# Decoder on one core: the first feed-forward with three batches open, its scratch stores on GpSimd, its norm on ScalarE and half of its rounding on VectorE

## The chip, the cores and the metric

The program is one kernel on one core of a Trainium2 chip. A core has a matrix engine (TensorE; PE in the profile, with its weight loads as PEld), three engines for elementwise work (VectorE = DVE, ScalarE = ACT, GpSimd = POOL), and SyncE (SP), which here only issues transfers. SBUF is the memory on the core that all engines read; PSUM holds eight banks of 128 x 512 fp32 into which TensorE writes; HBM is reached by DMA, which any engine but TensorE and VectorE issues here. Each engine runs its own instructions in one fixed order and waits on semaphores where it needs another's result.

The metric is device time in microseconds (us) of one execution. Each kernel is run several times, and the median counts. Besides, one execution is recorded by the hardware profiler; the views of that record are called the profile or the trace.

## The reference

A decoder of two layers on four batches of 512 tokens of width 512, in fp32. Each layer is attention, cross-attention and a feed-forward, and after each of them `x = layernorm(x + f(x))`. The change lies in the first layer's feed-forward (and in when the weights of the next attention are loaded):

```python
def act_quant(x):                       # per token, 8 bits
    scale = 128 / clip(max(abs(x), axis=-1), 1e-5)
    return clip(round(x * scale), -128, 127) / scale
def weight_quant(w):                    # ternary
    scale = 1 / clip(mean(abs(w)), 1e-5)
    return clip(round(w * scale), -1, 1) / scale
def bitlinear(x, w):   return einsum('bsh,oh->bso', act_quant(x), weight_quant(w))
def h_bitlinear(x, w): return einsum('bsh,oh->bso', act_quant(fwht(x)), weight_quant(w))
gate = bitlinear(x, w_gate)             # 512 -> 2048
up = bitlinear(x, w_up)                 # 512 -> 2048
x = layernorm(x + h_bitlinear(silu(gate) * up, w_down))   # 2048 -> 512
```

`fwht` is a normalised Walsh-Hadamard transform over the 2048 columns. `setup_inputs` makes random activations and weights.

## The kernel before

**Stages and order.** Six phases, A to F, are first attention, first cross-attention, first feed-forward (C, `l0_ffn`, L546), second attention (D), second cross-attention (E) and second feed-forward (F). Each runs on four batches 0 to 3; the result of a phase goes to HBM and the next phase loads it. Each phase of a batch is a generator that issues a few instructions and then yields. `lanes` (L1111) interleaves them: it takes the generators in the order A0 A1 ... F3 (L34), keeps at most two open, and opens the next when the last one opened has said "next" and the same batch has finished the phase before. Beside the named phases, `BESIDE` (L36) runs generators that prepare weights: while C3 and D0 are open, `l1_attn_weights` loads 16 `w1` tiles of the next attention's weights on SP, splits each into a high and a low part (ScalarE L135, VectorE L138) and folds a bias through TensorE (`bo1`).

The program's order of issue is then an input to a scheduler that fixes each engine's order of instructions; semaphores and the turn of the buffers (pools of 69 `o`, 13 `t`, 12 `x` and 4 `w` tiles of 256 KB, eight PSUM banks) are placed by it as well. A `Pipe` inside a generator delays a piece: `later(2, f)` calls `f` two ticks on, a tick being one step of the loop.

**One batch of the first feed-forward.** Names are those of the profile's rows.

1. Load four `x` tiles of 128 tokens; the maxima of each token and its scales go into a small tile `cm` (two buffers). Quantise (`qf` on ScalarE L569, `q` on VectorE), transpose to `qT`, and make `arow`, the row of token scales.
2. The front: 16 steps `o`, each a block of 128 hidden columns. A step has the matmuls of gate `pg` and up `pu` (four each, L624 and L626), then `g = pg * arow` (VectorE L595), silu (ScalarE L596), `g = pu * g` (VectorE L600), the split into `hh` (ScalarE L602) and `hl` (GpSimd L603), the first half of the Hadamard transform, a matrix product over the block's 128 columns with `hh` and then `hl` (L608 and L609, into `ph`), and a copy `hw` on ScalarE (L614). Two ticks later SP stores `hw`, 256 KB, to a scratch area in HBM (L615). There are two scratch areas, for even and odd batches. After step 6 the generator says "next".
3. The reload: after all 16 stores, 16 loads `z` on SP read the scratch with columns in another order (`z` number c takes 8 columns of each of the 16 blocks), so every load needs every store.
4. The back: for each of four token tiles, four groups of four matmuls `had` (the transform's second half, L692), each needing four `z`; the maximum of each group (VectorE L638) and a copy `q2f` (ScalarE L640); the scales, small operations on VectorE and one on GpSimd; rounding on ScalarE (L658), a subtraction and clip on VectorE (L659, `q`); eight transposes into `q2T` (L665), a copy (ScalarE L670), and the down product, 16 matmuls `dn` (L678); then the residual and the statistics of the layernorm on VectorE (L682).
5. `finish` (L180): the inverse root in small operations on VectorE (`ln_rsqrt`), `norm` on VectorE (L186), and the store of `x` on SP (L189). All six phases use it.

In the order that results, the fronts of batches 0 and 1 run, then both reloads, both backs; then the same for batches 2 and 3. The four last `dn` of batch 3 come before the second attention's score matmuls (`ds`, L835), which begin at 816.95 us.

**Lines that the change and the prediction touch.** L526 and L527 round weights (`tw`) on VectorE. Rows of the profile write out<-in: `had<-had,z` (L692) is the second half, `ph<-hh,had` the first.

Of the kernel before, what the change touches and what calls it, by code (L numbers as in the profile page):

```python
# [16 lines left out]
AF = mybir.ActivationFunctionType  # L17
ALU = mybir.AluOpType
# [4 lines left out]
P = 128  # L23
NT = 4
MAGIC = 12582912.0
RSQRT_SEED = float(0x5F3759DF)
O_BUFS, T_BUFS, X_BUFS, W_BUFS = 69, 13, 12, 4


D_NEXT = 7  # L30
B_NEXT = 13
F_LOAD = 5
# [32 lines left out]
class Net:  # L65
# [114 lines left out]
    def finish(self, pipe, ys, ln, phase, b):  # L180

        nc = self.nc
        self.ln_rsqrt(ln)

        def norm(i):
            nc.vector.tensor_scalar(ys[i], ys[i], ln[:, 2 * i : 2 * i + 1], ln[:, 24 + i : 25 + i], ALU.subtract, ALU.mult)  # L186

        def store(i):
            nc.sync.dma_start(self.xd[phase + 1][b, i * P : (i + 1) * P, :], ys[i])  # L189

        for i in range(NT):
            pipe.later(3, norm, i)
            pipe.later(4, store, i)
# [352 lines left out]
    def l0_ffn(self, b):  # L546
        nc = self.nc
        pipe = Pipe()
# [2 lines left out]
        yield  # L551
        yield

        cm = self.s("cm", 40, 2)
        am, a1, sc, cs, f2 = (cm[:, 4 * n : 4 * n + 4] for n in range(5))
        for i in range(NT):
            nc.vector.tensor_reduce(am[:, i : i + 1], x[i], AX.X, ALU.max, apply_absolute_value=True)
# [9 lines left out]
        for i in range(NT):  # L567
            f = self.t("qf")
# [22 lines left out]
        scratch = self.had_scratch[b % 2]  # L591
# [20 lines left out]
        def keep(o, ph):  # L612
            w = self.t("hw")
            nc.scalar.copy(w, ph)  # L614
            pipe.later(2, lambda: nc.sync.dma_start(scratch[o * P : (o + 1) * P, :], w))  # L615

        tern = self.tern
        for o in range(16):
            pipe.tick()
            c, m = o // 4, slice((o % 4) * P, (o % 4) * P + P)  # L620
            self.need("C", lambda: (3, c) in tern["wu_t"])
            pg, pu = self.pa("pg"), self.pa("pu")
            for k in range(NT):
                nc.tensor.matmul(pg, tern["wg_t"][k, c][:, m], qT[k], start=k == 0, stop=k == NT - 1)  # L624
            for k in range(NT):
                nc.tensor.matmul(pu, tern["wu_t"][k, c][:, m], qT[k], start=k == 0, stop=k == NT - 1)  # L626
            pipe.later(1, gate, o, pg, pu)
            yield "next" if o == 6 else None
        yield from pipe.drain()

        z = [self.load(self.o("z"), scratch.rearrange("(i c b) t -> c i b t", i=16, c=16)[c]) for c in range(16)]
        ln = self.ln_tile()
        yield
        yield
# [19 lines left out]
        def quant(i, half, fs, s2):  # L654
            q = self.t("q2", BF16, 1024)
            for g in range(2):
                f = fs[half * 2 + g]
                nc.scalar.activation(f, f, AF.Copy, bias=MAGIC, scale=s2)  # L658
                nc.vector.tensor_scalar(q[:, g * 512 : g * 512 + 512], f, MAGIC, 127.0, ALU.subtract, ALU.min)  # L659
            pipe.later(2, turn, i, half, q)  # L660

# [40 lines left out]
    def l1_attn_weights(self):  # L702
        nc, a = self.nc, self.a
# [13 lines left out]
        f = self.w("after")  # L717
# [6 lines left out]
        pipe = Pipe()  # L724
# [5 lines left out]

        for c, k, ap in order:
            pipe.tick()
            pipe.later(1, put, c, k, self.load(self.w("w1"), ap))
            yield
        yield from pipe.drain()

# [15 lines left out]
    def l1_attn(self, b):  # L752
# [75 lines left out]
        def scores(hh):  # L828
            q3, k3 = st.pop((0, hh)), st.pop((1, hh))
            p01, p2, p3 = self.pa("ds"), self.pa("ds"), self.pa("ds")  # L830
            place = ((p01, 0), (p01, 256), (p2, 0), (p3, 0))
            tiles = []
            for i, (ps, o) in enumerate(place):
                w = max(256, P * (i + 1))
                nc.tensor.matmul(ps[:, o : o + w], q3[:, i * P : (i + 1) * P], k3[:, 0:w], start=True, stop=True, skip_group_check=True)  # L835
                tiles.append(ps[:, o : o + P * (i + 1)])
            pipe.later(1, soft, hh, tiles)
# [47 lines left out]
        for hh in range(16):  # L885
# [5 lines left out]
            scores(hh)  # L891
            yield "next" if hh == D_NEXT else None
        yield from pipe.drain()
# [217 lines left out]
def lanes(order, task, step):  # L1111

    todo = [(e.strip("+!"), e[0] == "+", max(1, e.count("!"))) for e in order]
    plain = [name for name, _, _ in todo]
    live, done = {}, set()
    n, said = 0, 9
    while todo or live:
        if todo and len(live) < 2:  # L1120
            name, soon, times = todo[0]
            before = chr(ord(name[0]) - 1) + name[1]
            if (before in done or before not in plain) and (said >= times or not live or soon):
                todo.pop(0)
                live[name] = task(name)
                last = name
                n, said = n + 1, 0
        for name, g in list(live.items()):
            word = next(g, "end")
            if word == "end":  # L1130
                live.pop(name)
                done.add(name)
            elif word == "next" and name == last:
                said += 1
        step(n)
# [91 lines left out]
```

## Time and profile before

| | |
|---|---|
| median of 3 runs | 1662.6 us (1662.27 to 1663.54) |
| profiled execution | 1662.88 us, of it 1660.9 us from the first to the last instruction |
| mean granted TensorE clock | 0.978 of full speed |
| HBM read, written | 112.0 MB, 41.9 MB |

The first feed-forward runs from 479 to 799 us. Busy time of each engine in it and in the first part of the attention that follows, in us (the four stretches between 566 and 759 us that are not in this table are shown in the prediction):

| from-to, us | length | PE | DVE | ACT | POOL | granted clock | GB/s | what runs |
|---|---|---|---|---|---|---|---|---|
| 479-566 | 87 | 84.61 | 59.55 | 68.64 | 41.78 | 1.00 | 172 | fronts of batches 0 and 1 |
| 599-619 | 20 | 20.00 | 18.12 | 16.44 | 0.82 | 1.00 | 17 | backs of batches 0 and 1 |
| 759-799 | 40 | 39.29 | 28.81 | 29.36 | 7.84 | 1.00 | 56 | backs of batches 2 and 3 |
| 799-880 | 81 | 79.45 | 52.86 | 68.66 | 29.44 | 1.00 | 104 | second attention |

How to read it: the busy time of PE is modelled, since matmuls overlap, and an engine counts as busy while an instruction of it is open, so a full PE may still be doing its work at less than its peak. The granted clock is the share of TensorE's full clock that the chip allowed in that stretch. A row such as `pg<-qT,tb 128x512 bf16 x4` is a run of four instructions; the figures before it are its start and duration, and what stands in brackets behind it is the idle time before it and the work that ended that idle time. A DMA issue has two durations: that of the issuing instruction, and the time until the data landed. Over the stage, stores of `hw` have an issue of 0.32 us (median) and land 2.0 us after it; a `z` load lands 6.6 us after its issue (median, the 16 of a batch being queued together).

Mean durations of one instruction over the whole trace, for the operations that the change moves or that stand beside them:

| row | mean, ns | count |
|---|---|---|
| ACT L658 rounding `q2f` | 745 | 64 |
| DVE L659 `q<-q2f` | 419 | 64 |
| POOL L603 `hl` | 1323 | 64 |
| ACT L614 `hw` copy | 590 | 64 |
| DVE L186 `norm`, all phases | 687 | 96 |
| ACT L602 `hh` | 621 | 64 |

### The profile page before, as it was taken

To read this page: it belongs to the slowest core of one execution; us is meant where nothing else is said; L and a number is where in the kernel's file an instruction comes from. 1 tells how busy PE (TensorE), PEld (TensorE's weight loads), DVE (VectorE), ACT (ScalarE), POOL (GpSimd) and SP (SyncE) were. 2 spreads that over 40 slices of the span, in tenths; PEclk is the share of its full clock that TensorE was granted. 3 is DMA by queue.
4 is the path that set the end of the run, shared out by engine and by line. 5 is a ranking of instruction groups with operands and counts; after the bars stand their busy time and mean duration, and the time that the engine had idled before them with its cause. 6 is when DMAs were issued, how large, how long until landed. Compare 5 with 4: busy or idle time off the path is not lost.

```text
span 1660.9 us, 25661 instructions
## 1 busy us (share of the span) xinstructions
PE 1549.7 (93%) x8246; PEld 1110.3 (67%) x8246; DVE 1267.4 (76%) x2796; ACT 1007.5 (61%) x2149; POOL 667.4 (40%) x672
## 2 busy tenths in 40 slices
PE   7999999999999899899999999999988889999995
PEld 5888775444544674466777767777667766786874
DVE  6386688999976678876565675756879999979795
ACT  5333326888778867786696865968533445444542
POOL 5663653555535203420435332343323344333332
PEclk9999998999999999999999999999998999999998
DMA  7043343455114634763433323333444532021000
GB/s 243 28 146 121 127 133 118 144 165 184 58 71 146 193 114 138 205 188 98 127 77 77 77 64 109 83 77 77 153 152 123 189 106 63 9 69 47 5 26 25
DMA packets 103237, 180.77 MB, mean 109 GB/s; under 512 B 16560, under 2 KB 18608, under 8 KB 103104
## 3 DMA queue, kind: packets, MB, share of 16 engines
q1 hardware_dynamic: 98976, 170.69, 32.8%
q0 software_dynamic: 4128, 8.46, 2.1%
q8 instruction: 65, 1.06, 0.3%
q14 instruction: 68, 0.56, 0.1%
HBM read 111.98 MB, written 41.94 MB: 93 GB/s over the span
## 4 chain that ended last, share of the span: by engine, by line
PE 54%; DVE 23%; ACT 9%; DMA 7%; issue 4%; POOL 2%; SPq 1%; DVEq 0%; ACTq 0%; POOLq 0%
PE fg L1080 7%; PE facc L1071 6%; DVE bsm L413 3%; PE dT L857 2%; ACT de L847 2%; PE pu L626 2%; PE pg L624 2%; DVE x L186 2%; DMA z<-had_scratch 2%; DVE fg L1044 2%; PE dn L678 2%; PE dq L146 2%; PE dq L147 2%; PE dq L148 2%; PE do L877 2%
## 5 line engine op out<-in xcount | busy, mean ns | idle before, releaser
L1044 DVE SCALAR_TENSOR_TENSOR fg<-fg,gs,fg 128x512 f32<-128x512 f32 x220 | 162.4, 745 | 36.8 <-PE fg L1080 17.5
L1080 PE MATMUL fg<-fxh,gu 128*128 128x512 f32 x352 | 144.2, 410 | 7.5 <-DVE fg L1044 4.6
L847 ACT ACTIVATE de<-de,dm 128x128 f32<-128x128 f32 (+3 forms) x256 | 143.0, 563 | 13.4 <-DVE dm L846 12.4
L846 DVE CUSTOM_DVE_ANT_0 de<-ds,negm,thr 128x128 f32<-128x128 f32 (+3 forms) x256 | 126.5, 546 | 31.0 <-PE ds L835 27.9
L421 POOL TENSOR_SCALAR be<-be,bsm 128x512 f32<-128x512 f32 x128 | 95.7, 760 | 120.5 <-DVE bsm L419 70.4
L1080 PE MATMUL fg<-fxl,gu 128*128 128x512 f32 x352 | 139.2, 395 | 0.0
L603 POOL TENSOR_TENSOR hl<-g,hh 128x512 fp32r<-128x512 f32 x64 | 84.2, 1323 | 114.6 <-ACT hh L602 93.4
L1048 POOL TENSOR_TENSOR fg<-fg,fg 128x512 f32<-128x512 f32 x44 | 61.0, 1387 | 128.4 <-ACT fg L1041 69.5
L415 ACT ACTIVATE be<-bs,bsm 128x512 f32<-128x512 f32 x128 | 87.5, 690 | 39.3 <-DVE bsm L413 32.3
L777 POOL TENSOR_TENSOR dql<-dqf,dqh 128x512 fp32r<-128x512 f32 x32 | 41.4, 1295 | 154.5 <-ACT dqh L776 120.8
L857 PE MATMUL dT<-ident,de 128*128 128x128 f32 x640 | 89.9, 278 | 7.9 <-ACT de L847 5.9
L1080 PEld LDWEIGHTS fg<-fxh,gu 128*128 128x128 f32 x352 | 67.3, 191 | 38.1 <-DVE fg L1044 14.2
L857 PEld LDWEIGHTS dT<-ident,de 128*128 128x128 f32 x640 | 71.7, 141 | 25.6 <-ACT de L847 14.4
L1038 ACT ACTIVATE fg<-fg,gs 128x512 f32<-128x512 f32 x88 | 60.4, 686 | 39.1 <-PE fg L1080 38.6
L413 DVE TENSOR_REDUCE bsm<-bs 128x1 f32<-128x512 f32 x128 | 84.0, 674 | 0.1
L692 PE MATMUL had<-had,z 128*128 128x128 f32 x512 | 75.0, 293 | 9.5 <-DMA z<-had_scratch 9.3
L692 PEld LDWEIGHTS had<-had,z 128*128 128x128 f32 x512 | 68.9, 203 | 17.1 <-issue 6.4
L1071 PE MATMUL facc<-p4h,fhh 128*128 128x512 f32 x176 | 71.7, 409 | 8.9 <-DVE fg L1044 6.2
L437 PE MATMUL bo<-bpT,cT 128*64 128x512 f32 x256 | 75.4, 625 | 3.5 <-ACT bpT L428 1.5
L199 PEld LDWEIGHTS bT<-ident,be 128*128 128x128 f32 x512 | 55.1, 141 | 34.4 <-issue 12.9
L199 PE MATMUL bT<-ident,be 128*128 128x128 f32 x512 | 73.7, 283 | 3.9 <-POOL be L421 1.4
L1041 ACT ACTIVATE fg<-fg,gs 128x512 f32<-128x512 f32 x44 | 30.2, 687 | 75.1 <-PE fg L1080 75.1
(330 smaller groups left out, 4715.8 us busy)
## 6 DMA issues: line engine op xcount, KB each, us to landing
x<-x SPq DMA_DIRECT2D x176, 256.0 KB, 3.1
had_scratch<-hw SPq DMA_DIRECT2D x64, 256.0 KB, 2.0
z<-had_scratch SPq DMA_DIRECT2D x64, 256.0 KB, 6.6
stk<-dqh SPq DMA_DIRECT2D x192, 64.0 KB, 2.1
tw<-in_wg_t SPq DMA_DIRECT2D x32, 256.0 KB, 4.1
tw<-in_wu_t SPq DMA_DIRECT2D x32, 256.0 KB, 3.5
tw<-in_wd_t SPq DMA_DIRECT2D x32, 256.0 KB, 2.7
p<-in_gu_p SPq DMA_DIRECT2D x22, 256.0 KB, 2.7
```

The costliest lines, as they stand in the source:

```text
L199: self.nc.tensor.transpose(pt[:, i * P : (i + 1) * P], srcs[i][:, j * P : (j + 1) * P], self.ident)
L413: nc.vector.tensor_reduce(sm[:, h : h + 1], ps, AX.X, ALU.max, negate=True)
L415: nc.scalar.activation(e, ps, AF.Exp, bias=sm[:, h : h + 1], accum_out=sm[:, 2 + h : 3 + h])
L421: nc.gpsimd.tensor_scalar(es[h][i], es[h][i], sm[:, 4 + h : 5 + h], 1.0, ALU.mult, ALU.mult)
L603: nc.gpsimd.tensor_tensor(lo, g, hi.bitcast(F32), ALU.subtract)
L692: nc.tensor.matmul(ps[:, c * P : (c + 1) * P], z[g * 4 + c][:, i * P : (i + 1) * P], self.had16, start=True, stop=True)
L846: nc.vector.tensor_tensor_reduce(es[i], ps, self.negm[:, 384 - P * i :], -1.0, self.thr[:, i : i + 1], ALU.add, ALU.min, n4[:, i : i + 1])
L847: nc.scalar.activation(es[i], es[i], AF.Exp, bias=n4[:, i : i + 1], scale=-1.0, accum_out=den[:, hh * 4 + i : hh * 4 + i + 1])
L857: nc.tensor.transpose(pt[:, o + (i - j) * P : o + (i - j + 1) * P], es[i][:, j * P : (j + 1) * P], self.ident)
L1044: nc.vector.scalar_tensor_tensor(y[u], ps, s, y[u], ALU.mult, ALU.add)
L1071: nc.tensor.matmul(acc[t], h[l][:, c], self.dn[i][r], start=i == 0 and n == 0, stop=i == 10 and n == 2)
L1080: nc.tensor.matmul(ps, self.gu[i, u][:, g * P : (g + 1) * P], xT[g][n], start=n == 0, stop=n == 1)
```

## The change

In the first feed-forward:

- `lanes` lets three generators be open while the next one to open is a C; otherwise two, as before. The front says "next" after step 9 rather than 6.
- `finish` of this phase computes -mean x rstd for the four tiles in one small VectorE operation and normalises on ScalarE (`x * rstd + (-mean * rstd)`); the store of the result is issued by ScalarE rather than SP.
- The stores of `hw` to the scratch are issued by GpSimd rather than SP, one tick after the copy rather than two.
- Of the two halves of each token tile's rounding, the first runs on VectorE (multiply and add in one instruction) rather than ScalarE.
- `cm` has three buffers rather than two.

And the 16 `w1` loads of the next attention's weights are placed behind the latest `z` load in SP's order.

The changed order has the same instructions otherwise: 64 stores go from SP to GpSimd, 16 from SP to ScalarE, 16 norms from VectorE to ScalarE, 32 roundings from ScalarE to VectorE, and four small VectorE operations are new.

```diff
--- before.py
+++ after.py
@@ -27,6 +27,9 @@
 O_BUFS, T_BUFS, X_BUFS, W_BUFS = 69, 13, 12, 4
 
 
+C_NEXT = 9
+
+NORM_ACT = (2,)
 D_NEXT = 7
 B_NEXT = 13
 F_LOAD = 5
@@ -182,11 +185,19 @@
         nc = self.nc
         self.ln_rsqrt(ln)
 
+        on_act = phase in NORM_ACT
+        if on_act:
+
+            nc.vector.scalar_tensor_tensor(ln[:, 28:32], ln[:, 0:8].rearrange("p (i two) -> p i two", two=2)[:, :, 0], -1.0, ln[:, 24:28], ALU.mult, ALU.mult)
+
         def norm(i):
-            nc.vector.tensor_scalar(ys[i], ys[i], ln[:, 2 * i : 2 * i + 1], ln[:, 24 + i : 25 + i], ALU.subtract, ALU.mult)
+            if on_act:
+                nc.scalar.activation(ys[i], ys[i], AF.Identity, bias=ln[:, 28 + i : 29 + i], scale=ln[:, 24 + i : 25 + i])
+            else:
+                nc.vector.tensor_scalar(ys[i], ys[i], ln[:, 2 * i : 2 * i + 1], ln[:, 24 + i : 25 + i], ALU.subtract, ALU.mult)
 
         def store(i):
-            nc.sync.dma_start(self.xd[phase + 1][b, i * P : (i + 1) * P, :], ys[i])
+            (nc.scalar if on_act else nc.sync).dma_start(self.xd[phase + 1][b, i * P : (i + 1) * P, :], ys[i])
 
         for i in range(NT):
             pipe.later(3, norm, i)
@@ -551,7 +562,7 @@
         yield
         yield
 
-        cm = self.s("cm", 40, 2)
+        cm = self.s("cm", 40, 3)
         am, a1, sc, cs, f2 = (cm[:, 4 * n : 4 * n + 4] for n in range(5))
         for i in range(NT):
             nc.vector.tensor_reduce(am[:, i : i + 1], x[i], AX.X, ALU.max, apply_absolute_value=True)
@@ -612,7 +623,7 @@
         def keep(o, ph):
             w = self.t("hw")
             nc.scalar.copy(w, ph)
-            pipe.later(2, lambda: nc.sync.dma_start(scratch[o * P : (o + 1) * P, :], w))
+            pipe.later(1, lambda: nc.gpsimd.dma_start(scratch[o * P : (o + 1) * P, :], w))
 
         tern = self.tern
         for o in range(16):
@@ -625,10 +636,11 @@
             for k in range(NT):
                 nc.tensor.matmul(pu, tern["wu_t"][k, c][:, m], qT[k], start=k == 0, stop=k == NT - 1)
             pipe.later(1, gate, o, pg, pu)
-            yield "next" if o == 6 else None
+            yield "next" if o == C_NEXT else None
         yield from pipe.drain()
 
         z = [self.load(self.o("z"), scratch.rearrange("(i c b) t -> c i b t", i=16, c=16)[c]) for c in range(16)]
+        self.reload = self.loaded
         ln = self.ln_tile()
         yield
         yield
@@ -655,7 +667,10 @@
             q = self.t("q2", BF16, 1024)
             for g in range(2):
                 f = fs[half * 2 + g]
-                nc.scalar.activation(f, f, AF.Copy, bias=MAGIC, scale=s2)
+                if half:
+                    nc.scalar.activation(f, f, AF.Copy, bias=MAGIC, scale=s2)
+                else:
+                    nc.vector.tensor_scalar(f, f, s2, MAGIC, ALU.mult, ALU.add)
                 nc.vector.tensor_scalar(q[:, g * 512 : g * 512 + 512], f, MAGIC, 127.0, ALU.subtract, ALU.min)
             pipe.later(2, turn, i, half, q)
 
@@ -730,7 +745,8 @@
 
         for c, k, ap in order:
             pipe.tick()
-            pipe.later(1, put, c, k, self.load(self.w("w1"), ap))
+            with self.tc.issue_after(self.reload.ins):
+                pipe.later(1, put, c, k, self.load(self.w("w1"), ap))
             yield
         yield from pipe.drain()
 
@@ -1117,7 +1133,7 @@
     live, done = {}, set()
     n, said = 0, 9
     while todo or live:
-        if todo and len(live) < 2:
+        if todo and len(live) < (3 if todo[0][0][0] == "C" else 2):
             name, soon, times = todo[0]
             before = chr(ord(name[0]) - 1) + name[1]
             if (before in done or before not in plain) and (said >= times or not live or soon):
```

## The prediction

> **What bounds the kernel now.** I read the totals first, then the busy time by stretch of the first feed-forward (the only stage whose instruction order the change moves, apart from its seam with the attention that follows), then TensorE's timeline there, then the chain of waits at the two holes.
>
> ```profile
> PE 1549.7 (93%) x8246; PEld 1110.3 (67%) x8246; DVE 1267.4 (76%) x2796; ACT 1007.5 (61%) x2149; POOL 667.4 (40%) x672
> ```
>
> TensorE is the busiest engine, but its busy time is modelled, so I count its work from rows instead. The stage runs from 479.5 us (first gate matmul) to 798.6 us (last down matmul), 319.1 us.
>
> ```profile
> core 0: us, PE busy (x) PEld busy (x) DVE busy (x) ACT busy (x) POOL busy (x), PEclk, DMA share, GB/s
> 566.00:599.00 33.00, 27.63 (x173) 20.15 (x172) 17.40 (x45) 21.21 (x35) 0.85 (x3) 0.84 0.53 153
> 619.00:705.00 86.00, 77.81 (x383) 39.47 (x382) 75.12 (x148) 65.10 (x113) 33.76 (x26) 0.98 0.57 178
> 705.00:729.00 24.00, 24.00 (x156) 16.53 (x156) 20.31 (x42) 19.46 (x37) 10.80 (x10) 1.00 0.64 204
> 729.00:759.00 30.00, 25.87 (x161) 18.72 (x160) 16.13 (x40) 19.77 (x33) 0.56 (x2) 0.89 0.61 169
> ```
>
> The reader is to see two stretches in which every engine falls back at once, GpSimd to nothing, and the granted clock drops to 0.84 and 0.89. Between them TensorE is full beside DVE at 85%. What a piece of work costs TensorE is the distance from one start to the next where nothing waits:
>
> ```profile
> 497.85 1.04 PE L624 MATMUL pg<-qT,tb 128*128 128x512 bf16 x4
> ...
> 500.04 1.04 PE L624 MATMUL pg<-qT,tb 128*128 128x512 bf16 x4
> ...
> 603.29 3.62 PE L678 MATMUL dn<-tb,q2T 128*128 128x512 bf16 x16
> 606.74 0.61 PE L665 MATMUL q2T<-ident,q 128*128 128x128 bf16 x8
> 607.19 2.90 PE L692 MATMUL had<-had,z 128*128 128x128 f32 x24
> 609.92 3.62 PE L678 MATMUL dn<-tb,q2T 128*128 128x512 bf16 x16
> ```
>
> One front step (gate, up, first Hadamard half) is 2.19 us, a tile of `dn` 3.45, eight transposes 0.45, eight records of `had` 0.91. Four batches: 64 x 2.19 = 140.2, 64 x 0.91 = 58.2, 16 x 3.45 = 55.2, 32 x 0.45 = 14.4; `arow` and `qT` of three batches 5.5, the bias fold `bo` 4.2 (697.50 to 701.73), attention work let in at the end 4.6. Sum 282.3, so about 37 of 319 us are lost. The same count inside the stretches (88 `had`, 48 `dn`, 40 transposes in the first hole, 22.6 us of work in 33) gives 10.4 us lost in the first, 9.4 in the second and 11.9 in 619 to 705.
>
> ```profile
> 572.27 3.42 DMA had_scratch<-hw
> ...
> 578.24 5.39 DMA z<-had_scratch
> ...
> 583.70 7.46 DMA z<-had_scratch
> 591.16 0.14 issue
> ```
>
> The holes are the round trip through scratch: the last store of a batch lands, only then its 16 loads start.
>
> ```profile
> 575.75 11.27 SPq L203 DMA_DIRECT2D z<-had_scratch  x16
> ...
> 579.24 0.77 PE L692 MATMUL had<-had,z 128*128 128x128 f32 x2 [3.92 <-DMA z<-had_scratch]
> ```
>
> First load issued 575.75, first `had` 579.24 (3.5 us), sixteenth load used at 594.75: one load per (594.75 - 579.24) / 15 = 1.03 us. Both batches of a pair have finished their fronts by then, so nothing is left to run.
>
> **The change part by part.** The sum is made against the profiled execution, 1662.9 us (span 1660.9 and 2.0 around it); the median is 1662.6.
>
> *Three batches open, "next" at step 9.* In the changed order on TensorE, `had` of batch 0 stands between steps of batch 1, that of batch 1 between steps of batch 2, that of batch 2 between steps of batch 3. The pair's common hole goes: -10.4 and -9.4. Of the 11.9 us in 619 to 705, 5.5 stand around the bias fold (TensorE waits 2.90 us before 697.50, DVE splitting attention weights) and stay, since the fold still falls into batch 3's front; the other 6.4 are the restart of two fronts on drained engines, which now happens inside another batch's back: -6.4. Together -26.2. The later "next" costs nothing: batch 1's first step stands after batch 0's last Hadamard halves, and at 512 to 517.8 TensorE already waits there for `qT`.
>
> *What it adds there.* Four reloads instead of two pairs. From the last Hadamard matmul to the last of 16 loads: matmul and copy 0.25 + 0.1 + 0.6, store 2.3 with issue, first load 3.5, fifteen more 14.3 to 15.5: 21.4 us taken. Batch 0's reload stands beside five steps of batch 1 (5 x 1.74 = 8.7 us before the first `had`, against 6.8 for the first load), then a group of four loads takes 3.8 to 4.1 us where a step with its `had` group takes 3.1: +2 (0 to 7). Batch 1's has about 13 us of batch 2's steps before its first `had`: 0 (0 to 4). Between batch 2's last half and batch 3's first gate matmul TensorE's order holds 4.5 of `had`, two `dn` (6.9), 40 transposes (2.3), `arow` and `qT` (1.9): 15.6 against 21.4, +6 (0 to 10). After batch 3's last half stand one `dn` (3.45) and `had` of two tiles (7.3) before the attention's first transpose: 10.8 against 21.4 and 2 for the second tile, +12.6 (8 to 17).
>
> *The seam.* Attention's first transpose then comes with about 17 us more of batch 3's back still to do than before. Two of its four `dn` with their transposes (2 x 3.9) stand among the score matmuls of 817 to 880, where TensorE loses 2 to 5 us in each 10; they are hidden there: -7 (0 to -8). If that cover is gone they cost 7.
>
> *GpSimd issues 64 stores.* No 256 KB store from GpSimd is in the trace. Its `had` load of 64 KB took 0.74 us of the engine and landed after 2.29; the 32-partition copies took 0.50. Bounds 0.50 and four times 0.74, 2.95; taken 0.8, by the row with 128 partitions. 51 us go onto an engine that has 95 of 318 busy: hidden, because a store and a split (0.8 + 1.28) stay under a step of 2.19. At 2.95 they don't, and the split `hl` behind a store, which the Hadamard matmul waits for, sets a step of 4.2. SP loses 64 issues of 0.32; loads no longer hold stores back as at 542.29 to 546, where a store waits for landings of loads. That block had no TensorE cost of its own: 0 (0 to -3).
>
> The DMA issue itself comes second. The Trainium skill (DMA: Bandwidth & Descriptors, "Issuing engine by pattern") gives simple stores to Sync, and states about 1 us to the first byte for GpSimd against 0.6. The rows above have 2.29 against 2.0 to landing. By the page's difference the four last stores would cost 4 x 0.4 = 1.6 us, by the rows 4 x 0.3; neither is in the sum.
>
> *Half of the rounding on DVE, norm on ScalarE, its stores too.* 32 roundings leave ScalarE (0.72 each, median of L658, -23.0) and go to DVE at 0.48, the row of `tw` L526, the same multiply and add (+15.4). 16 norms leave DVE (1.92 / 4 = 0.48, -7.7) for ScalarE at 0.72, the rounding's form (+11.5); 16 issues on ScalarE, none in this trace, by SP's rows 0.32 to 0.72, taken 0.34 (+5.4). ScalarE -6.1, DVE +7.7; both have over 75 us spare in the stage, so 0 by themselves. The issues wait for their norm with the next copies queued behind, and for their semaphore's earlier load: bounds 0 and 11.5.
>
> *DVE beside GpSimd.* This speaks against the change. The same four norms:
>
> ```profile
> 616.78 1.92 DVE L186 TENSOR_SCALAR x<-x,ln 128x512 f32<-128x512 f32 x4
> ...
> 647.47 2.86 DVE L186 TENSOR_SCALAR x<-x,ln 128x512 f32<-128x512 f32 x4
> ```
>
> ```profile
> 643.23 3.02 POOL L603 TENSOR_TENSOR hl<-g,hh 128x512 fp32r<-128x512 f32 x2 [2.02 <-ACT hh L602]
> 648.28 1.31 POOL L603 TENSOR_TENSOR hl<-g,hh 128x512 fp32r<-128x512 f32 x1 [2.02 <-ACT hh L602]
> ```
>
> GpSimd is idle beside the first and splits beside the second: 0.24 us more each. Backs so far ran mostly with GpSimd idle; now 64 `q`, 32 roundings and small steps run beside splits: 96 x 0.24 = 23 us of DVE. That is covered by DVE's spare 80 us except in batch 3's stretch, where 12 weight splits share DVE (about 65 us of DVE to 67 of TensorE): +3 (0 to 23).
>
> The Trainium skill (GPSIMD Engine Reference, "Key points") says that GpSimd shares its SBUF interfaces with VectorE, with contention for DVE instructions that use both ports or read two SBUF operands. The rows agree. The page has no price; by it alone every such pair would contend, at the rows' price the 23 us.
>
> *The rest.* Weight loads behind a reload and a third `cm` buffer move no TensorE work: 0 (-2 to +4).
>
> Sum: -26.2 + 2 + 0 + 6 + 12.6 - 7 + 3 = -9.6, **1653 us**.
>
> **Rivals.** (a) *Reload paces TensorE's fixed order in all four batches: slower.* For it: a hole's loads already run at 1.03 us each with no other traffic, and now another batch's stores share the DMA. With a group of loads at 4.8 us, batches 0 to 3 lose 7, 4, 10 and 17: 38 instead of 20.6. 1662.9 - 26.2 + 38 - 7 = 1668. It decides where a group takes over 4.2 us, a step with its share of the back (2.19 + 0.91 + 3.45/4 + 0.22). Against: 705 to 729 moves 204 GB/s with TensorE full. (b) *The hole only moves to batch 3 and DVE binds its stretch: no change.* DVE's contention at 13 instead of 3: 1663. Against: DVE at 85% in 705 to 729 costs nothing. (c) *Reloads hidden better:* batch 2's under batch 1's `dn`, batch 3's at its lower bound, the rest 0: 1662.9 - 26.2 + 8 - 7 = 1638.
>
> **How the numbers follow.** Main case 0.46, with a range of its own of 1645 to 1661; (a) 0.27; (b) 0.13; (c) 0.14. I predict 1653; the range 1636 to 1676 reaches into (c) and past (a) by its last bound. A measurement of this kernel tells 0.2% (3.3 us) from no change. Faster: 0.41 of the main case and (c), with a little of (b): 0.56. Same 0.13. Slower 0.31, from (a) and the edges of (b).
>
> **What would show it.** TensorE without a hole while batches 1 and 2 run their fronts; `had` of batch 2 and of batch 3 waiting on `z`, about 6 and 12 us; GpSimd's stores near 0.8 us; `q` and the roundings 0.2 us longer beside `hl`; attention's first transpose near 770 us and its score matmuls a few us earlier than 817. Wrong would be: `had` waiting on `z` in all four batches, GpSimd setting the step, or score matmuls later than 817 with TensorE stopped behind DVE or ScalarE.

## The result, and the profile after

The changed kernel takes 1712.0 us (median of 4 runs, 1711.7 to 1713.1) beside 1663.1 us for the kernel before; the ratio is 1.0288, with a 95% interval of 1.0269 to 1.0308. It is slower by about 48 us. The prediction was 1653 us with a range up to 1676: wrong in sign and in size. The profiled execution took 1713.1 us, of it 1711.4 us from the first to the last instruction, at a mean granted clock of 0.967 (0.978 before).

The totals of the changed kernel, from the page:

```profile
PE 1579.3 (92%) x8246; PEld 1121.0 (66%) x8246; DVE 1281.3 (75%) x2816; ACT 997.1 (58%) x2133; POOL 707.2 (41%) x736
```

TensorE has the same 8246 matmuls as before and 50.5 us more span (1711.4 - 1660.9). No engine became full: the time went into waits. Four stretches of the changed kernel, between its first gate matmul of the feed-forward (482 us) and the attention's first score matmul (842 us):

```profile
core 0: us, PE busy (x) PEld busy (x) DVE busy (x) ACT busy (x) POOL busy (x), PEclk, DMA share, GB/s
...
600.00:640.00 40.00, 40.00 (x248) 24.38 (x247) 31.58 (x71) 26.53 (x46) 17.20 (x20) 1.00 0.50 156
640.00:680.00 40.00, 28.39 (x176) 19.57 (x174) 25.50 (x64) 23.63 (x41) 9.66 (x13) 0.86 0.71 214
680.00:720.00 40.00, 33.46 (x198) 21.78 (x198) 31.36 (x73) 27.21 (x45) 7.52 (x8) 0.84 0.36 106
...
760.00:800.00 40.00, 30.14 (x150) 19.85 (x147) 18.38 (x46) 16.44 (x28) 8.35 (x12) 0.79 0.63 204
```

The first of the two holes of before is gone, as meant: TensorE is full from 600 to 640, and it was not in 566 to 599 before. But there are two others, longer ones, at 640 to 720 and at 760 to 800, again with a lower granted clock (down to 0.79). What TensorE waited for between 479 and 930 us (in all, times, longest):

```profile
engine line waited for: us in total, times, longest us
PE had L707 <- DMA z<-had_scratch: 16.7, 15, 6.1
PE dn L693 <- ACT q2T L685: 8.8, 1, 8.8
PE bo L761 <- DVE bvp L758: 3.5, 1, 3.5
PE q2T L680 <- DVE q L674: 2.4, 1, 2.4
```

Two stretches show how. The first, after batch 2's last Hadamard half, as the timeline has it (start, duration, engine; in brackets the wait before):

```profile
643.22 0.82 ACTq L200 DMA_DIRECT2D x<-x  x2
...
645.30 7.39 SPq L214 DMA_DIRECT2D x<-x  x4
...
659.10 0.63 ACT L625 COPY hw<-ph 128x512 f32<-128x512 f32 x1
660.02 0.59 POOL L626 DMA_DIRECT2D had_scratch<-hw  x1 [1.31 <-ACT hw L625]
...
662.42 10.74 SPq L214 DMA_DIRECT2D z<-had_scratch  x16
...
666.00 0.77 PE L707 MATMUL had<-had,z 128*128 128x128 f32 x2 [6.12 <-DMA z<-had_scratch]
...
672.95 1.89 PE L693 MATMUL dn<-tb,q2T 128*128 128x512 bf16 x8
673.55 16.17 SPq L214 DMA_DIRECT2D w<-in_wqkv  x7
...
682.07 0.62 ACT L138 CAST w1h<-w 128x512 fp32r<-128x512 f32 x1 [15.73 <-DMA w<-in_wqkv]
...
683.66 3.60 PE L693 MATMUL dn<-tb,q2T 128*128 128x512 bf16 x8 [8.82 <-ACT q2T L685]
...
691.33 1.03 PE L635 MATMUL pg<-qT,tb 128*128 128x512 bf16 x4
```

Read it from the top. Batch 0 stores its result at 643.22, and only then (645.30) does batch 3 load its `x`: three batches may be open, so batch 3 opens when batch 0 is done. Batch 2's last first half (its last `ph`) ends at 654.5; ScalarE copies it only at 659.10, GpSimd issues its store at 660.02, the 16 loads start at 662.42, and the last of them lands at 681.60. Batch 3's first gate matmul comes at 691.33: for 36.8 us there is no front to cover batch 2's reload. TensorE waits 6.1 us for `z`. Then ScalarE waits 15.7 us, to 682.07, for a `w1` tile whose load stands behind the 16 `z` loads on SP; the copy of `q2T` is queued behind that split, and half of a `dn` waits 8.8 us for it.

The second stretch is batch 3's reload:

```profile
770.50 3.63 PE L693 MATMUL dn<-tb,q2T 128*128 128x512 bf16 x16
...
778.54 1.74 PE L707 MATMUL had<-had,z 128*128 128x128 f32 x4 [4.42 <-DMA z<-had_scratch]
...
780.70 4.44 ACTq L200 DMA_DIRECT2D x<-x  x3
785.18 0.59 ACT L652 COPY q2f<-had 128x512 f32<-128x512 f32 x1 [3.79 <-DMA z<-had_scratch]
...
791.86 6.24 PE L707 MATMUL had<-had,z 128*128 128x128 f32 x40 [0.15 <-DMA z<-had_scratch]
797.94 0.60 PE L210 MATMUL dx<-ident,x 128*128 128x128 f32 x4
```

From 773.95 (end of the last `dn`) to 797.94 TensorE does 64 records of `had`, 7.3 us of work at the prediction's price (64 x 0.91 / 8), so 16.7 us are lost. ScalarE's three last result stores start at 780.70, 783.27 and 784.81, each 0.07 to 0.08 us after the landing of a `z` load (780.62, 783.20, 784.74) whose semaphore it reuses; a `q2f` copy stands behind them.

A count over the whole stage, made as in the prediction (the distance from start to start where nothing waits is work, the rest is idle), in two halves: from the first gate matmul to 639 to 642 us, and from there to the attention's first score matmul.

| kernel | idle, first half | idle, second half | first gate to first score | attention's scores 1 to 64 |
|---|---|---|---|---|
| before | 19.6 | 25.9 | 337 | 84 |
| changed | 15.2 | 57.4 | 359 | 109 |
| three open alone (e3) | 11.4 | 48.9 | 340 | 106 |
| GpSimd's stores alone (e10) | 27.7 | 36.7 | 351 | 84 |
| e17 (batch 3's back kept out of the attention) | 11.2 | 51.5 | 350 | 88 |

So the loss is 22 us up to the first score (359 - 337), which comes at 841.7 instead of 816.95, and another 28 in the second attention (from its first score matmul to the last feed-forward's first matmul, 522 us, before 494). From there to the end the two are alike (347.5 and 349.7).

### The profile page after: what moved, and what is told of

Same layout as the page of the kernel before. It is cut to its first block, busy times and chain, and to the rows that moved or that the text cites. A ratio compares the mean times of both kernels' runs of the same rounds, so it can differ in the third digit from the quotient of the medians.

```text
span 1711.4 us, 25656 instructions
## 1 busy us (share of the span) xinstructions
PE 1579.3 (92%) x8246; PEld 1121.0 (66%) x8246; DVE 1281.3 (75%) x2816; ACT 997.1 (58%) x2133; POOL 707.2 (41%) x736
## 5 line engine op out<-in xcount | busy, mean ns | idle before, releaser
L1060 DVE SCALAR_TENSOR_TENSOR fg<-fg,gs,fg 128x512 f32<-128x512 f32 x220 | 162.3, 745 | 34.3 <-PE fg L1096 15.7
L862 DVE CUSTOM_DVE_ANT_0 de<-ds,negm,thr 128x128 f32<-128x128 f32 (+3 forms) x256 | 126.2, 546 | 44.2 <-PE ds L851 38.8
L426 ACT ACTIVATE be<-bs,bsm 128x512 f32<-128x512 f32 x128 | 87.6, 691 | 38.8 <-DVE bsm L424 31.7
L873 PE MATMUL dT<-ident,de 128*128 128x128 f32 x640 | 96.4, 283 | 12.1 <-ACT de L863 9.6
L707 PE MATMUL had<-had,z 128*128 128x128 f32 x512 | 83.0, 305 | 19.6 <-DMA z<-had_scratch 16.7
L707 PEld LDWEIGHTS had<-had,z 128*128 128x128 f32 x512 | 73.7, 211 | 31.9 <-DMA z<-had_scratch 14.4
L1096 PEld LDWEIGHTS fg<-fxh,gu 128*128 128x128 f32 x352 | 66.3, 188 | 39.3 <-DVE fg L1060 15.6
L1054 ACT ACTIVATE fg<-fg,gs 128x512 f32<-128x512 f32 x88 | 60.4, 687 | 39.9 <-PE fg L1096 39.4
L309 POOL TENSOR_TENSOR z<-z,rope_cos 128x512 f32<-128x512 f32 x32 | 46.0, 1449 | 72.8 <-DVE zs L307 59.6
```

The costliest lines, as they stand in the source:

```text
L426: nc.scalar.activation(e, ps, AF.Exp, bias=sm[:, h : h + 1], accum_out=sm[:, 2 + h : 3 + h])
L707: nc.tensor.matmul(ps[:, c * P : (c + 1) * P], z[g * 4 + c][:, i * P : (i + 1) * P], self.had16, start=True, stop=True)
L862: nc.vector.tensor_tensor_reduce(es[i], ps, self.negm[:, 384 - P * i :], -1.0, self.thr[:, i : i + 1], ALU.add, ALU.min, n4[:, i : i + 1])
L873: nc.tensor.transpose(pt[:, o + (i - j) * P : o + (i - j + 1) * P], es[i][:, j * P : (j + 1) * P], self.ident)
L1060: nc.vector.scalar_tensor_tensor(y[u], ps, s, y[u], ALU.mult, ALU.add)
L1096: nc.tensor.matmul(ps, self.gu[i, u][:, g * P : (g + 1) * P], xT[g][n], start=n == 0, stop=n == 1)
```

## The experiments

Differences in us are (ratio - 1) x 1663, each against runs of the kernel before on the same chip. A difference between two rows of the table carries the errors of both: with the half widths of the two intervals added as squares it is known to 4 to 8 us.

| run | what | median, us | ratio [95%] | us |
|---|---|---|---|---|
| changed | all of it | 1712.0 | 1.0288 [1.0269, 1.0308] | +47.9 |
| e1 | changed, `w1` loads not behind the reload | 1711.8 | 1.0277 [1.0236, 1.0319] | +46.1 |
| e2 | changed, two open | 1683.2 | 1.0114 [1.0076, 1.0153] | +19.0 |
| e4 | changed, stores on SP | 1700.8 | 1.0219 [1.0175, 1.0264] | +36.4 |
| e8 | changed, attention's batch 1 as a third | 1703.5 | 1.0253 [1.0232, 1.0274] | +42.1 |
| e11 | changed, norm on VectorE, its stores on SP | 1703.1 | 1.0245 [1.0229, 1.0262] | +40.7 |
| e12 | changed, rounding on ScalarE | 1718.7 | 1.0335 [1.0319, 1.0352] | +55.7 |
| e16 | changed, norm's stores on SP | 1702.6 | 1.0230 [1.0204, 1.0255] | +38.2 |
| e3 | before, three open | 1688.3 | 1.0142 [1.0107, 1.0177] | +23.6 |
| e5 | e3, attention's batch 1 as a third | 1679.3 | 1.0100 [1.0076, 1.0124] | +16.6 |
| e9 | e5, `w1` loads issued by GpSimd | 1679.4 | 1.0098 [1.0081, 1.0116] | +16.3 |
| e17 | e3, attention opens after all of C | 1680.9 | 1.0106 [1.0071, 1.0140] | +17.6 |
| e6 | before, next after step 9 | 1661.7 | 1.0004 [0.9992, 1.0016] | +0.7 |
| e7 | changed, two open, next after step 6 | 1669.9 | 1.0050 [1.0032, 1.0067] | +8.3 |
| e10 | before, stores on GpSimd | 1677.1 | 1.0083 [1.0064, 1.0103] | +13.8 |
| e13 | before, stores on GpSimd, two ticks | 1672.2 | 1.0050 [1.0030, 1.0069] | +8.3 |
| e14 | before, stores on SP, one tick | 1662.9 | 0.9997 [0.9983, 1.0011] | -0.5 |
| e15 | before, half of the rounding on VectorE | 1661.7 | 0.9984 [0.9969, 0.9998] | -2.7 |
| e18 | e15 and the norm on ScalarE, stores on SP | 1663.3 | 0.9989 [0.9972, 1.0007] | -1.8 |

### Which part: the open batches, the stores, the weights

e1, two lines of the change undone:

```diff
-            with self.tc.issue_after(self.reload.ins):
-                pipe.later(1, put, c, k, self.load(self.w("w1"), ap))
+            pipe.later(1, put, c, k, self.load(self.w("w1"), ap))
```

> The changed kernel with the 16 w1 loads no longer placed behind the reload. Theory 1 (the loads of the next attention's weights, late behind 16 z loads, stop ScalarE for 15.7 us and TensorE for 8.8 us behind it): that wait goes and the kernel is 10 to 20 us faster than the changed one, 1692 to 1702 us. Theory 2 (the order with three batches open is itself the loss, the stall only fills time that the reload would take anyway): at most 4 us faster, 1708 to 1712 us.

e2 (changed) and e3 (before, with the third `cm` buffer and next after step 9):

```diff
# e2; e3 is the reverse
-        if todo and len(live) < (3 if todo[0][0][0] == "C" else 2):
+        if todo and len(live) < 2:
```

> The changed kernel with two generators open instead of three; everything else of the change stays (next after step 9, GpSimd's stores, half of the rounding, the norm, w1 loads behind the reload). Theory 1 (w1 loads): the stall stays, 1675 to 1700 us. Theory 2 (the order with three open costs, by batch 3's reload and by its back inside the second attention): 1655 to 1670 us, about the kernel before. Theory 3 (GpSimd's stores and DVE's contention): over 1690 us.

> The kernel before with three batches open, next after step 9 and a third cm buffer, and nothing else. Theory 2: 1690 to 1712 us, most of the loss. Theory 1 and 3: it has the gain of the holes without their cost, 1640 to 1665 us.

e4:

```diff
-            pipe.later(1, lambda: nc.gpsimd.dma_start(scratch[o * P : (o + 1) * P, :], w))
+            pipe.later(2, lambda: nc.sync.dma_start(scratch[o * P : (o + 1) * P, :], w))
```

> The changed kernel with the scratch stores back on SP, two ticks after the copy. Theory 3 (GpSimd's issue at 0.6 us and its splits in one queue make the front slower): 5 to 20 us faster, 1692 to 1707 us. Theory 1 and 2: within 5 us of the changed kernel, 1707 to 1717 us, or slower where SP's queue holds a store behind waiting loads.

Three open batches alone cost 23.6 us, and taking them out of the changed kernel gives 28.9 back: half of the loss or a little more, where theory 2 had most of it. Without the explicit placement the time hardly moves, as theory 2 expected and theory 1 did not; but ScalarE's wait for `w1` is still 9.8 us, since the loads of a background generator come behind the reload in SP's order by themselves (in e3 it is 8.8 us), so that e1 alone doesn't settle theory 1. Run e9 below takes the wait away. Of theory 3 the price of the stores holds beside theory 2: SP's stores give 11.5 back. e3 came 1.7 us under theory 2's band. e2 landed in theory 1's band and not in theory 2's, but not for theory 1's reason: no wait of ScalarE for `w1` is in its trace. What it still has are the stores and the later next:

e6 is the kernel before with next after step 9, e7 is e2 with next after step 6:

```diff
# e6; e7 is the reverse
-            yield "next" if o == 6 else None
+            yield "next" if o == 9 else None
```

> The kernel before with next after step 9 rather than 6, and nothing else. Theory C (a later next takes the pair of batches apart, so that one front and one reload stand alone): 1672 to 1684 us, most of what e2_two_open lost. Theory D (GpSimd's stores, the norm, the rounding or the w1 loads lost it): 1660 to 1667 us, no change.

> The changed kernel with two generators open and next after step 6: only GpSimd's stores, ScalarE's norm, half of the rounding on VectorE and the w1 loads behind the reload are left of the change. Theory C: 1658 to 1668 us. Theory D: 1675 to 1685 us, as e2_two_open.

The later next alone costs nothing, so theory C falls for e6. With the other edits it costs 10.7 us (e2 against e7), and those alone 8.3: e7 lies between the bands of C and D. So the later next and the other edits work on each other, and how is not settled.

### Why three open lengthen the attention

e5 on e3, e8 on the changed kernel:

```diff
-        if todo and len(live) < (3 if todo[0][0][0] == "C" else 2):
+        if todo and len(live) < (3 if todo[0][0][0] == "C" or todo[0][0] == "D1" else 2):
```

> The three open batches alone (as in e3_lanes_only), and the second attention's batch 1 may also open as a third generator. Theory A (batch 3's back lives so long that the limit of two keeps the attention's batch 1 out, and batch 0 runs alone on a chain that leaves TensorE idle): the attention's batch 1 begins its transposes 30 us or more earlier than 899 us, and the kernel is 15 to 28 us faster than e3_lanes_only, 1660 to 1673 us. Theory B (the work of batch 3's back inside the attention's scores is what slows them): 1680 to 1692 us, as before.

> The whole change, and the second attention's batch 1 may open as a third generator. Theory A: 15 to 28 us faster than the changed kernel, 1684 to 1697 us. Theory B: 1705 to 1714 us.

e17 on e3:

```diff
-        if todo and len(live) < (3 if todo[0][0][0] == "C" else 2):
+        if todo and len(live) < (3 if todo[0][0][0] == "C" else 1 if todo[0][0] == "D0" else 2):
```

> Three batches open alone (as e3_lanes_only), but the second attention's batch 0 opens only when all four batches of the feed-forward are done, so that batch 3's back stands alone. From the first to the 64th score matmul the attention takes 84 us again, as in the kernel before (106 us in e3_lanes_only); that is what the work inside it and the closed door cost together. Theory S (the work gets no cover in the attention's scores): the first score matmul comes 15 to 25 us later than 820 us and the time stays within 6 us of 1688 us. Theory T (the scores cover some of it, as the prediction had it): 1695 us or more.

The timeline of e3 where batch 3's last `dn` ends and the attention's batch 1 begins with its transposes `dx`:

```profile
859.55 3.61 PE L678 MATMUL dn<-tb,q2T 128*128 128x512 bf16 x15
898.58 0.44 PE L199 MATMUL dx<-ident,x 128*128 128x128 f32 x2
```

The same in e5, and the first `dx` of batch 1 in the kernel before:

```profile
858.21 3.61 PE L678 MATMUL dn<-tb,q2T 128*128 128x512 bf16 x15
876.79 0.60 PE L199 MATMUL dx<-ident,x 128*128 128x128 f32 x4
```

```profile
858.94 0.60 PE L199 MATMUL dx<-ident,x 128*128 128x128 f32 x4
```

The attention's batch 1 stayed out until batch 3 of the feed-forward was done, 40 us later than before; opened as a third it comes 22 us earlier, and the times fall by 7.0 us (e3 to e5, known to 7) and 5.8 us (changed to e8, known to 5). That is theory A at about a third of its size; e17 shows what the rest is. Busy time over the first 64 score matmuls, before, in e3, in e5 and in e17:

```profile
817.00:900.00 83.00, 81.45 (x544) 63.40 (x542) 49.65 (x155) 69.08 (x190) 35.39 (x50) 1.00 0.32 77
```

```profile
820.00:927.00 107.00, 100.45 (x620) 72.20 (x621) 66.52 (x190) 77.51 (x202) 36.70 (x50) 0.98 0.30 80
```

```profile
819.00:919.00 100.00, 94.05 (x604) 68.97 (x605) 59.49 (x183) 75.98 (x200) 36.82 (x51) 1.00 0.32 85
```

```profile
831.00:919.00 88.00, 84.79 (x553) 65.06 (x554) 52.78 (x160) 72.91 (x197) 35.88 (x51) 1.00 0.35 87
```

The 17 us between 83 and 100 in e5 hold 60 matmuls more; from there on its attention is like the kernel before (115, 88 and 67 us for the next quarters in both). In e17 batch 3's back is out, and the stretch falls to 88. But e17 lifts the closed door as well: the attention's batch 1 begins 46 us after the first score matmul (877.4 after 831.25), near the 42 of before and far from the 78 of e3. So the 6.0 us between e3 and e17 (known to 8) are door and work together. What the work alone costs is read, as near as these runs allow, between e5 (batch 1 after 58 us) and e17. From the first score matmul to the last feed-forward's first matmul e5 takes 508.8 us and e17 498.1, 10.7 less; its first score matmul comes 12.2 us later (831.25 against 819.0); and the two times are 1.0 us apart (known to 7). So, in these traces, the work of batch 3's back costs about as much inside the attention as by itself: the idle time there covers 1 to 2 of about 12 us. Theory T falls. Theory S had that right, with a smaller delay than it expected (10.9 us after e3's first score) and a time 1 us below its band, since the open door came with it.

### Weights from another queue

e9 on e5:

```diff
-            pipe.later(1, put, c, k, self.load(self.w("w1"), ap))
+            w = self.w("w1")
+            nc.gpsimd.dma_start(w, ap)
+            pipe.later(1, put, c, k, w)
```

> As e5_lanes_d1 (three batches open, attention's batch 1 as a third), with the 16 w1 loads issued by GpSimd, so that they don't stand behind batch 2's 16 z loads in SP's queue. Theory M (in every order with three open, ScalarE waits 7 to 16 us for a w1 tile queued behind the reload, and TensorE behind ScalarE): ScalarE's wait for in_wqkv falls under 2 us and the time by 4 to 9 us, to 1670 to 1675 us. Rival (TensorE waits for z and for batch 3's late front at the same place, so that the wait is only replaced): within 3 us of 1679 us, as undoing the explicit placement gave nothing in e1_w1free.

ScalarE's wait for `in_wqkv` is gone from the list (7.4 us in e5), and the time is the same (0.3 us, known to 5): no gain shows, and theory M falls. In its place ScalarE waits 6.0 us for the transposes `qT`; TensorE waits for `z` as before (6.2 us, 6.0 in e5). The 15.7 us in the changed kernel's timeline looked like the largest single cause, and neither e1 nor e9 shows any time in such a wait. The trace fits the rival: in the changed kernel the wait ends at 682.07, and batch 2's last `z` lands at 681.60, so that without the wait TensorE would lack this `z` and batch 3's front all the same.

### GpSimd's stores

e10 and e13 (one and two ticks on GpSimd), e14 (one tick on SP), all on the kernel before:

```diff
-            pipe.later(2, lambda: nc.sync.dma_start(scratch[o * P : (o + 1) * P, :], w))
+            pipe.later(1, lambda: nc.gpsimd.dma_start(scratch[o * P : (o + 1) * P, :], w))  # e10
+            pipe.later(2, lambda: nc.gpsimd.dma_start(scratch[o * P : (o + 1) * P, :], w))  # e13
+            pipe.later(1, lambda: nc.sync.dma_start(scratch[o * P : (o + 1) * P, :], w))    # e14
```

> The kernel before with GpSimd issuing the scratch stores one tick after the copy, and nothing else. If the stores cost what e4_sp_stores gave back (11 us) by themselves: 1670 to 1676 us. If they cost only where fronts run beside backs: 1661 to 1667 us.

> The kernel before with GpSimd issuing the scratch stores two ticks after the copy, as SP did. Theory Q (a store one tick after its copy waits in GpSimd's queue for the copy, with the next split behind it): the loss of e10_pool_stores_only goes, 1660 to 1667 us, and GpSimd's wait of stores for hw falls from 23 us to under 8. Theory I (0.57 us of issue on GpSimd for each step, or the slower way of the store, whatever its place): 1671 to 1679 us.

> The kernel before with its scratch stores on SP one tick after the copy instead of two, and nothing else. If the tick moves the order of the whole front by itself: 1668 us or more. Under theories Q and I: 1658 to 1666 us.

The stores' group in e10 (busy, mean ns of one; then the idle time before them and what ended it), and the same wait in e13:

```profile
L615 POOL DMA_DIRECT2D had_scratch<-hw x64 | 36.1, 564 | 29.5 <-ACT hw L614 23.1 <-PE had L692 2.7 <-PE pu L626 1.5
```

```profile
POOL had_scratch L615 <- ACT hw L614: 19.6, 15, 3.7
```

A store costs GpSimd 0.56 us, less than the 0.8 taken, and GpSimd is far from full; even so the stores cost 13.8 us in the order of the kernel before, 1 us over the larger of the two expectations. The tick explains about 5 of it on GpSimd (13.8 to 8.3; the intervals of the two runs just overlap) and nothing on SP (e14). Theory Q falls as the main cause: at two ticks GpSimd still waits 19.6 us for `hw`, and 8.3 us stay. The fronts of the four batches, from the first to the last `ph` pair, take 37.3, 38.0, 40.5 and 45.4 us before, 38.8, 42.4, 42.7 and 49.5 in e10, and 38.6, 38.1, 42.7 and 47.9 in e13. All four fronts are longer in e10, and three of them in e13, so the loss is not in one place. The median store lands 2.4 us after its issue in e10 and 2.6 in e13 (2.0 on SP), which accounts for little. Why the remaining 8 us arise is not settled.

The Trainium skill (DMA: Bandwidth & Descriptors, "Issuing engine by pattern") gives simple loads and stores to Sync and calls that path generally faster. The runs agree, and put the price here at 8.3 to 13.8 us for 64 stores.

### The norm and the rounding

```diff
# e11
-NORM_ACT = (2,)
+NORM_ACT = ()
# e16
-            (nc.scalar if on_act else nc.sync).dma_start(self.xd[phase + 1][b, i * P : (i + 1) * P, :], ys[i])
+            nc.sync.dma_start(self.xd[phase + 1][b, i * P : (i + 1) * P, :], ys[i])
# e12 (and, the other way, e15 on the kernel before)
-                if half:
+                if True:
                     nc.scalar.activation(f, f, AF.Copy, bias=MAGIC, scale=s2)
```

> The changed kernel with the norm back on VectorE and its stores on SP. Theory N (a norm on ScalarE and four issues behind it stand in front of copies that TensorE waits for): 1698 to 1708 us. Rival (ScalarE has room): 1709 to 1715 us.

> The changed kernel with all rounding back on ScalarE. Theory R (VectorE, full in batch 3's stretch beside weight splits and GpSimd, delays the steps): 1700 to 1708 us. Rival (the rounding is covered, as predicted): 1709 to 1715 us.

> The kernel before with the first half of each tile's rounding on VectorE, and nothing else. From e12_act_round (undoing it costs 7 us): 1653 to 1659 us, faster than the kernel before. If VectorE's room is only there in the changed order: 1661 to 1667 us.

> The changed kernel with the norm on ScalarE and its stores issued by SP. If the issues and their waits on ScalarE cost what e11_dve_norm gave back: 1701 to 1707 us. If it is the norm's own time on ScalarE: 1709 to 1715 us.

e18 is the kernel before with e15's rounding, ScalarE's norm and SP's stores of it.

> The kernel before with half of the rounding on VectorE and the norm on ScalarE with its stores still on SP (third cm buffer kept, it has no part in this): the two edits of the change that cost nothing so far. If they add up: 1652 to 1660 us, faster than both kernels. If the holes of the reload bound the pair of batches whatever the two engines do: 1660 to 1666 us.

Giving only the 16 issues back to SP returns 9.7 us (e16), as much as giving back the whole norm (7.2, e11). So the norm on ScalarE costs nothing that shows, and its DMA issues do. One way in which they cost stands in the timeline at 780 us: three of batch 3's four issues start only when an earlier load on their semaphore has landed, and ScalarE, with a copy queued behind them, stands idle for 3.8 us. But that is the smaller part. From batch 3's last first half to the attention's first transpose e16 gains 1.2 us (26.1 against 27.3), while up to the first score matmul it gains 7.8 (351.7 against 359.5) and in the attention 6.5 (515.7 against 522.2). How 16 issues cost that much is not shown.

The rounding on VectorE is a gain in the changed kernel (7.8 us slower without it, which neither expectation had), and next to none in the kernel before (-2.7 us, at the edge of what can be told). VectorE pays for it beside GpSimd. The group of `q` in the changed kernel's feed-forward (62 of its 64), and in the kernel before:

```profile
L674 DVE TENSOR_SCALAR q<-q2f 128x512 bf16<-128x512 f32 x62 | 33.2, 578 | 0.0
```

```profile
L659 DVE TENSOR_SCALAR q<-q2f 128x512 bf16<-128x512 f32 x64 | 26.0, 419 | 16.6 <-ACT q2f L658 16.6
```

Of the changed kernel's 64 `q`, 45 ran with GpSimd idle for at least half of their time (mean 0.417 us) and 19 beside it (0.942); of its 32 roundings 20 (0.480) and 12 (0.909). That is 19 x 0.525 + 12 x 0.429 = 15 us of VectorE, below the 23 that the prediction counted, and still the rounding gains.

No combination was faster than the kernel before by more than can be told: e15 and e18 are within 0.2% of it, and e18's interval includes 1.

## Why the prediction was wrong, point by point

**The holes, -26.2.** Right for the first pair, by the three open batches alone: 8.2 us of idle time less in the first half (19.6 to 11.4 in e3; the terms there were -10.4 and +2). Wrong for the second pair: idle time there rose from 25.9 to 48.9 in e3 and to 57.4 in the changed kernel, where the terms -9.4, -6.4, +6 and +12.6 made +2.8. This is the step that failed most.

Behind it stands a reading of the order before. The description of the kernel puts both reloads of a pair behind both fronts, and the prediction counted "four reloads instead of two pairs". But the kernel before already ran batch 0's `had` between batch 1's steps, and batch 2's between batch 3's (from 703.93 on):

```profile
538.75 1.05 PE L692 MATMUL had<-had,z 128*128 128x128 f32 x8
539.56 0.48 PE L608 MATMUL ph<-hh,had 128*128 128x512 f32 x1
...
541.85 1.05 PE L692 MATMUL had<-had,z 128*128 128x128 f32 x8
```

So the two holes of before were the reloads of batches 1 and 3 alone. The change covers batch 1's with batch 2's front, uncovers batch 2's, and leaves batch 3's open: there are two open reloads again.

The term that was furthest off here is +6, for the stretch between batch 2's last first half and batch 3's first gate matmul. The prediction set 15.6 us of work there against a reload of 21.4. The stretch took 36.8 us (35.8 in e3), so about 21 us in it are idle. The first wait for `z`, 6.1 us, agrees with the 6 by chance: it is one of several losses. The reload took 27.1 us (654.5 to 681.60), since the last copy waited on ScalarE to 659.10, and batch 3's front was not ready when the reload ended: batch 3 opens only when batch 0 is done, and its transposes `qT` stand on TensorE behind the wait for `z`, its `arow` on ScalarE behind the `w1` wait. Which of these sets the 691.33 is not shown. Batch 3's reload at 16.7 us lies inside its bounds of 8 to 17. And the steps after a wait can run at a lower clock (eight `dn` matmuls at 683.66 take 3.60 us, where 16 otherwise take 3.62).

**The seam, -7.** The second failed step. Two `dn` were taken as hidden, since TensorE loses 2 to 5 us in each 10 there. Two of batch 3's four `dn` do come behind the first score matmul, and they are not hidden: taking the work out shortened the attention by 10.7 us and delayed its first score by 12.2 (e5 to e17). That idle time gave next to no cover. And the prediction missed that a longer life of batch 3 keeps the attention's batch 1 out: 6 to 7 us (e5, e8). The prediction compared the order only up to the score matmuls of the attention's batch 0; the rest of that phase changed too, and it grew by 28 us. The attention's first transpose came at 797.94 us, where the prediction looked for it near 770.

**GpSimd's stores, 0.** The engine time was taken at 0.8 and was 0.57 in the changed kernel; the argument that 0.8 + 1.28 fits under a step of 2.19 compares busy time, and the cost is not there. By themselves they cost 13.8 us.

**Norm and rounding, 0 by themselves.** The bounds for ScalarE's issues were 0 and 11.5, and the lower one was taken; the runs say 9.7 (known to 5). The rounding is worth about 8 us in this kernel, which was not forecast.

**VectorE beside GpSimd, +3.** The mechanism and the size of each (0.24 taken; 0.53 and 0.43 measured, on 31 instructions rather than 96) are there; whether any of it reaches the end is not shown.

**Weight loads behind the reload, 0 (-2 to +4).** Right in time (1.8 us when undone, with an interval of 7 us on either side), though not for the reason given: a stall of 15.7 us is there, and it ends half a microsecond after the reload does.

The undone parts of the changed kernel sum to 28.9 + 11.5 + 7.2 + 1.8 - 7.8 = 41.6 of 47.9 us. The rest is within what these intervals leave open, if the parts add; e2 beside e6 and e7 shows that not all of them do. Rival (a), the one that ended slower, gave 1668 us for a reload that paces TensorE in all four batches; it did so in two, and more than half of the loss was in the attention, which no rival named.

## What to carry to other kernels

Before a third piece of work is opened, write down what has to finish before the fourth may open, and what covers the second transfer in that gap; a hole that is filled at the front can come back at the end, and there it also pushes work into the next phase. Idle time of an engine is not room until that is tested: move the work out of it, as near as you can with nothing else changed, and see whether the time grows (here, e5 against e17, it did not). And an issue of a transfer is not priced by the busy time of the engine that issues it: here 64 stores on GpSimd and 16 on ScalarE cost 8 to 14 and about 10 us on engines that were 41% and 58% busy.

## What was not expected of the hardware

A DMA issue on ScalarE starts within 0.1 us of the landing of an unrelated load on another queue, when both use one semaphore (landing and start: 780.62 and 780.70, 783.20 and 783.27, 784.74 and 784.81 us). The largest single wait of ScalarE in the stage, 15.7 us, could be shortened (9.8 in e1) or taken away (e9, against e5's 7.4) for nothing in the time that could be told. And a move that adds no instruction, 64 issues from SP to GpSimd at the same tick, costs 8.3 us.
